# Attention and FFN block on one core: the second eight heads' q and k projected in their own batch, the next batch's norm begun nine turns later, the normalisation of attention on GpSimd

## The chip, the cores and the metric

The kernel runs on one core of a Trainium2 chip. The metric is device time in microseconds (us); a figure for a kernel is the median of several runs. A profile is one further execution, recorded instruction by instruction. The engines are TensorE (PE in the profile; its weight loads are PEld), VectorE (DVE), ScalarE (ACT), GpSimd (POOL) and SyncE (SP), which here only issues DMAs. Each engine works through its own instructions in the order in which the program wrote them, and waits where an operand or a buffer is not ready.

## The reference

Four sequences of 1024 tokens with 256 features go through an attention block and a gated FFN, each on a layer-normed input, and each result is layer-normed again before it is added:

```python
x = x + _layernorm(_L0_attn_ref(_layernorm(x), Wqkv, Wout))
x = x + _layernorm(_L0_ffn_ref(_layernorm(x), ...))

# attention, 16 heads of 16 features
qkv = (x @ Wqkv.T).reshape(B, S, 3, H, Dh)
scores = jnp.einsum('bhqd,bhkd->bhqk', q, k) * scale
exp_x = jnp.exp(jnp.clip(x - x_max, -50.0, 50.0))
attn = exp_x / (jnp.sum(exp_x, axis=-1, keepdims=True) + EPS)
out = jnp.einsum('bhqk,bhkd->bhqd', attn, v)      # then @ Wout.T

# FFN, 1024 hidden, ternary weights with a scale for each output
h = jax.nn.silu(_tlin(x, w1_w, w1_s)) * _tlin(x, w2_w, w2_s)
h = jax.nn.gelu(_tlin(h, h1_w, h1_s), approximate=False)
h = jax.nn.gelu(_tlin(h, h2_w, h2_s), approximate=False)
return _tlin(h, w3_w, w3_s)
```

All of it is float32.

## The kernel before

**Two stages.** Attention runs over all four batches first, then the FFN over eight halves of 512 tokens. The kernel is a fast path that assumes that scores stay small enough for a softmax without the maximum and that the FFN's weights are exact in a rounded float format. Both assumptions are tested on the way, and a slow path runs if one fails.

**Units, tiles, chunks.** A batch has 16 heads in four groups g of four. A group's queries are split in two halves h of 512; a group and a half make a unit. A unit is 16 tiles: eight chunks c of 128 keys, and for each chunk two tiles u of two heads each. A tile is two matmuls into PSUM (L457) and one exponential over 1024 elements on ScalarE (L458). When both tiles of a chunk are ready, four matmuls weigh the chunk (L465): they multiply the exponentials with the values and accumulate in `acc`. VectorE keeps a running maximum `top` of the first 128 queries' exponentials (L474), because the reference's EPS is scaled by it. There are 512 tiles in all, 128 in a batch.

**Turns.** The main loop (L874) goes by turns of three tiles. In each it makes up to three tiles, lets VectorE take up finished chunks into `top`, weighs one or two chunks whose exponentials are behind it, and then calls `side.take()` (L569) once. PSUM holds three tiles (pool `ps`, three buffers), so PE can be at most one turn ahead of ScalarE. At a unit's end (L600) VectorE copies `acc` to `o`, and the weighing of the next unit is put off to the next turn.

**Side work.** Everything else is cut into `Step`s in chains. `side.take()` goes over the chains in `first` and then in `rest`. Of each it takes steps from the front while `gap` turns have passed since that chain's last one. Only one step of a turn may use TensorE, and a chain whose next step would be the second waits. Nearly all of these steps share one PSUM buffer (`misc`, one buffer), which VectorE must have emptied before the next one.

The steps of attention are:

- `divide` (L476), once a unit, in `first`: transposes `top` and `o` on PE, then normalises on VectorE. It borrows one of the three score buffers, and the next turn makes a tile less at its start.
- `ending` (L501), appended to the unit's chain at the last group: two transposes of the result (`oT`), two output projections (`py`), two gathers of statistics, a root (the reciprocal root by a GpSimd `pow`, L103), two applies (L539, the normalisation (x - mean) * rstd, two instructions of 128x256 each), two residual additions (L546).
- `prologue` (L276) of the next batch: for each half, gathers and a root (lists `norm`), then two applies into `xn` (L302) and two transposes into `xT` (`xt`). After that come the q and k projections (L325), each 16 short matmuls and two evictions on VectorE, in two sets `qk[0]` and `qk[1]` for the first and the second eight heads (m = 0, 1). Then there are four steps `values` (`pv`). The steps `flags` test the scores' size: `total` (a reduction of 1024 elements on VectorE), `squares` (ScalarE, L344), `bound` (`pn`: four small matmuls and a reduction on VectorE, L367), `gauge` and `flag` (`pr`).
- `check_weights` (L236): loads a block of FFN weights on the GpSimd queue, rounds it on GpSimd (a cast of 128x1024), counts differences on VectorE, stores it.

**The order before.** `begin(b)` (L589) is called when batch b begins. It builds the whole prologue of batch b+1, and puts its norms, transposes and `qk[0]` in one chain, without delay except in batch 0. At the end of group 1, `unit_end` appends `values` to that chain, and adds a second chain that waits five turns and then does `qk[1]` and the flags. So both projection sets of batch b+1 are made while batch b runs, and `flags` runs over into batch b+1. Batch 0 also makes its own `qk[1]`, since before the loop only its `qk[0]` is made.

**Copies.** At a unit's end with h = 1, `stack` (L425) issues 32 DMAs of 64 KB on SP that lay out q and k of the group after next, and `slots` (L431) copies that group's values on GpSimd.

## Time and profile before

| | us |
|---|---|
| median of 3 runs | 1326.66 (1326.26 to 1327.31) |
| the profiled execution's own time | 1328.08 |
| its span, first to last instruction | 1326.3 |
| first exponential of batch 0 | 28.38 |
| last weighing of batch 3, about | 649.2 |

In the profiled execution TensorE was busy for 95% of the span, VectorE for 55%, ScalarE for 53% and GpSimd for 9%:

```profile
PE 1264.8 (95%) x8194; PEld 777.2 (59%) x8194; DVE 723.2 (55%) x1561; ACT 697.0 (53%) x847; POOL 120.5 (9%) x166
...
PE   7889999999999999889999999999999999999996
PEld 3333333333333333333478888888888888888885
DVE  3575669756696556646573543636436263362523
ACT  3687788877887787988641422414123141231410
POOL 5221112101121000000010000000000000000000
```

The rows below the dots cut the span in 40 equal slices (33 us each) and give the busy tenths of each. Attention is slices 1 to 20 and the FFN the rest. PE is nearly always busy, but a busy PE is not one at its peak: matmuls are pipelined and the profile models their ends. In attention ScalarE is at 7 to 9 tenths as well. A time by turns, read from ScalarE's rows, says more than these shares.

### The profile page before, as it was taken

To read this page: it belongs to the slowest core of one execution; us is meant where nothing else is said; L and a number is where in the kernel's file an instruction comes from. 1 tells how busy PE (TensorE), PEld (TensorE's weight loads), DVE (VectorE), ACT (ScalarE), POOL (GpSimd) and SP (SyncE) were. 2 spreads that over 40 slices of the span, in tenths; PEclk is the share of its full clock that TensorE was granted. 3 is DMA by queue.
4 is the path that set the end of the run, shared out by engine and by line. 5 is a ranking of instruction groups with operands and counts; after the bars stand their busy time and mean duration, and the time that the engine had idled before them with its cause. 6 is when DMAs were issued, how large, how long until landed. Compare 5 with 4: busy or idle time off the path is not lost.

```text
span 1326.3 us, 21103 instructions
## 1 busy us (share of the span) xinstructions
PE 1264.8 (95%) x8194; PEld 777.2 (59%) x8194; DVE 723.2 (55%) x1561; ACT 697.0 (53%) x847; POOL 120.5 (9%) x166
## 2 busy tenths in 40 slices
PE   7889999999999999889999999999999999999996
PEld 3333333333333333333478888888888888888885
DVE  3575669756696556646573543636436263362523
ACT  3687788877887787988641422414123141231410
POOL 5221112101121000000010000000000000000000
PEclk8999999999999999999999999999999999999998
DMA  4665444444444333334230000000000000000000
GB/s 127 156 184 128 102 97 116 118 112 121 105 110 110 68 64 65 59 63 166 81 112 0 1 16 1 17 0 6 11 0 17 0 17 0 0 17 0 17 0 20
DMA packets 38670, 79.76 MB, mean 60 GB/s; under 512 B 11296, under 2 KB 21152, under 8 KB 38560
## 3 DMA queue, kind: packets, MB, share of 16 engines
q1 hardware_dynamic: 30672, 53.66, 18.4%
q0 software_dynamic: 7360, 24.12, 5.6%
q8 instruction: 67, 1.10, 0.4%
q10 hardware_dynamic: 528, 0.52, 0.1%
q14 instruction: 43, 0.35, 0.1%
HBM read 28.98 MB, written 15.73 MB: 34 GB/s over the span
## 4 chain that ended last, share of the span: by engine, by line
PE 75%; DVE 12%; ACT 8%; issue 2%; DMA 1%; SPq 1%; ACTq 0%; POOL 0%; POOLq 0%; DVEq 0%
PE ph L703 35%; PE acc L465 12%; PE s L457 8%; ACT e L458 7%; PE pz L756 4%; PE p L268 4%; PE pg L703 4%; PE py L268 2%; DVE top L474 2%; PE pv L268 2%; DVE sg L719 2%; PE po L486 1%; DVE ha_lo L708 1%; DVE o L274 1%; DVE st L93 1%
## 5 line engine op out<-in xcount | busy, mean ns | idle before, releaser
L458 ACT ACTIVATE e<-s 128x1024 f32<-128x1024 f32 x512 | 486.3, 1035 | 121.7 <-PE s L457 109.0
L465 PE MATMUL acc<-e,vaug 128*32 128x512 f32 x2048 | 255.1, 600 | 1.4 <-POOL vaug L435 1.4
L739 ACT ACTIVATE a<-ph,h_scale 128x512 f32<-128x512 f32 x128 | 81.1, 686 | 306.9 <-PE ph L703 306.9
L457 PE MATMUL s<-sq,sk 64*128 64x512 f32 x1024 | 194.0, 449 | 25.5 <-ACT e L458 22.6
L703 PE MATMUL ph<-hb_lo,h 128*128 128x512 f32 x512 | 199.4, 389 | 0.0
L703 PE MATMUL ph<-hb_hi,h 128*128 128x512 f32 x512 | 199.4, 389 | 0.0
L457 PEld LDWEIGHTS s<-sq,sk 64*128 64x128 f32 x1024 | 86.6, 184 | 164.7 <-ACT e L458 126.9
L474 DVE TENSOR_TENSOR top<-top,e 128x512 f32<-128x512 f32 x192 | 133.6, 696 | 35.7 <-ACT e L458 30.2
L740 DVE CAST ha_hi<-a 128x512 fp32r<-128x512 f32 x64 | 27.1, 423 | 157.9 <-ACT a L739 157.9
L465 PEld LDWEIGHTS acc<-e,vaug 128*32 128x32 f32 x2048 | 49.2, 108 | 106.1 <-issue 97.3
L103 POOL TENSOR_TENSOR rstd<-ve,minus_half 128x4 f32<-128x4 f32 (+1 forms) x33 | 37.5, 1137 | 791.1 <-DVE ve L101 791.1
L703 PEld LDWEIGHTS ph<-hb_lo,h 128*128 128x128 f32 x512 | 96.1, 188 | 20.1
L703 PEld LDWEIGHTS ph<-hb_hi,h 128*128 128x128 f32 x512 | 96.1, 188 | 20.2
L703 PE MATMUL ph<-ha_hi,sq 128*128 128x512 f32 x256 | 101.9, 398 | 0.4
L703 PE MATMUL ph<-ha_lo,sq 128*128 128x512 f32 x256 | 99.9, 390 | 0.0
L703 PE MATMUL ph<-ha_lo,sk 128*128 128x512 f32 x256 | 99.8, 390 | 0.0
L703 PE MATMUL ph<-ha_hi,sk 128*128 128x512 f32 x256 | 99.7, 390 | 0.0
L719 DVE SCALAR_TENSOR_TENSOR sg<-pg,w_scale,sg 128x512 f32<-128x512 f32 x64 | 47.1, 745 | 48.4 <-ACT sg L717 48.4
L717 ACT ACTIVATE sg<-pg,w_scale 128x512 f32<-128x512 f32 x64 | 43.4, 689 | 57.2 <-DVE ha_lo L708 48.4
L740 DVE CAST hb_hi<-a 128x512 fp32r<-128x512 f32 x64 | 27.0, 422 | 82.3 <-ACT a L739 82.3
L268 PE MATMUL p<-xT,wqk_sb 128*32 128x512 f32 x512 | 62.3, 608 | 0.9 <-ACT xT L271 0.9
L703 PEld LDWEIGHTS ph<-ha_hi,sq 128*128 128x128 f32 x256 | 48.2, 188 | 12.7 <-DVE sg L719 3.4
(145 smaller groups left out, 1642.9 us busy)
## 6 DMA issues: line engine op xcount, KB each, us to landing
w<-in_h_dram POOLq DMA_DIRECT2D x16, 512.0 KB, 4.5
h_r<-wr POOLq DMA_DIRECT2D x16, 512.0 KB, 3.8
sk<-ck1hi SPq DMA_DIRECT2D x64, 64.0 KB, 2.3
sk<-ck1lo SPq DMA_DIRECT2D x64, 64.0 KB, 2.3
sq<-cq1hi SPq DMA_DIRECT2D x64, 64.0 KB, 2.3
sq<-cq1lo SPq DMA_DIRECT2D x64, 64.0 KB, 2.3
h<-h_r SPq DMA_DIRECT2D x8, 512.0 KB, 7.1
sk<-ck0hi SPq DMA_DIRECT2D x56, 64.0 KB, 2.3
```

The lines of the kernel that those rows point to most:

```text
L103: nc.gpsimd.tensor_tensor(rstd[:, :n], ve[:, :n], self.minus_half[:, :n], ALU.pow)
L268: nc.tensor.matmul(o[j : j + SLOT, :], w[:, j : j + SLOT], i, **flags)
L457: nc.tensor.matmul(s[:, a, :], stacks[1, g % 2, u][r, c * P : (c + 1) * P], stacks[0, g % 2, u][r, h * NQ : (h + 1) * NQ], start=True, sto ...
L458: nc.scalar.activation(pair(k)[:, u], s, AF.Exp)
L465: nc.tensor.matmul(acc[SLOT * i : SLOT * (i + 1), :], vaug[g % 2][:, c, i, :], pair(k)[:, i // 2, i % 2, :], start=c == 0, stop=c == NT - 1)
L474: nc.vector.tensor_max(top, top if c > 1 else pair(k - 2)[:, :, :, 0:P], pair(k)[:, :, :, 0:P])
L703: nc.tensor.matmul(p, homes[n][c][:, m * P : (m + 1) * P], half[:, c, :], start=c == 0 and k == 0, stop=c == len(homes[n]) - 1 and k == 1)
L717: nc.scalar.activation(sg, p[:, 0, :], AF.Silu, scale=scales["w1"][:, m : m + 1])
L719: nc.vector.scalar_tensor_tensor(sg, p[:, 1, :], scales["w2"][:, m : m + 1], sg, ALU.mult, ALU.mult)
L739: nc.scalar.activation(a, p[:, j, :], AF.Gelu, scale=scales[n][:, m : m + 1])
L740: nc.vector.tensor_copy(o[0][:, m, :], a)
L756: nc.tensor.matmul(p[t], half[:, c, t * P : (t + 1) * P], homes["w3"][c], start=c == 0 and k == 0, stop=c == HC - 1 and k == 1)
```

## The change

Three things are changed, and one follows from them.

1. **The second projections.** `prologue(b + 1)` is still built in `begin(b)`, but its `qk[1]` is kept in `own` and carried out when batch b+1 itself begins. It is a chain of four projections put in front of all others (`first=None`), two turns apart (one in batch 0). The chain's last step, `go_on`, then adds the flags of the second eight heads, and extends the chain of the next batch by its transposes, `qk[0]` and the flags of its first eight heads.
2. **The norm.** The chain of the next batch starts with nine turns of waiting instead of none (batch 0: four, as before), and does gathers and roots of both halves in a row. `values` has a chain of its own from the end of group 1, and the slots copy of the next batch's group 0 follows it where it is not done by then.
3. **The normalisation.** `Norms.apply` takes an engine. In `ending`, and in `prologue` of batches 1 to 3, the 128x256 instruction that subtracts and multiplies is issued on GpSimd; it was on VectorE.
4. **The flags** are split by m: `bound(m, h)` does two matmuls and a reduction over half of the partitions, so `pn` takes a PE step four times in a batch instead of twice. The small tiles `norm`, `sum` and `sum2` get two buffers.

```diff
-    def apply(self, o, t, stats, i):
+    def apply(self, o, t, stats, i, engine=None):
         mv, rstd = stats
-        self.nc.vector.tensor_scalar(o, t, mv[:, i, 0:1], rstd[:, i : i + 1], ALU.subtract, ALU.mult)
+        (engine or self.nc.vector).tensor_scalar(o, t, mv[:, i, 0:1], rstd[:, i : i + 1], ALU.subtract, ALU.mult)
...
-                        norms.apply(st["xn"][:, i, :], rows(h)[i], st["ln", h], i)
+                        norms.apply(st["xn"][:, i, :], rows(h)[i], st["ln", h], i, None if b == 0 else nc.gpsimd)
...
-            def bound(h):
+            def bound(m, h):
                 def run():
-                    pn = space(f"pn_{b}_{h}")
-                    for k, (w, m) in enumerate(kinds):
-                        nc.tensor.matmul(pn[SLOT * k : SLOT * (k + 1), :], heads_bf, st["sq", w, m], start=True, stop=True)
-                    nc.vector.tensor_reduce(st["norm"][:, TPQ * h : TPQ * (h + 1)], pn.rearrange("p (t n) -> p t n", n=P), AX.X, ALU.max)
+                    pn = space(f"pn_{b}_{m}_{h}")
+                    for w in range(2):
+                        nc.tensor.matmul(pn[SLOT * (2 * m + w) : SLOT * (2 * m + w + 1), :], heads_bf, st["sq", w, m], start=True, stop=True)
+                    own = slice(2 * SLOT * m, 2 * SLOT * (m + 1))
+                    nc.vector.tensor_reduce(st["norm"][own, TPQ * h : TPQ * (h + 1)], pn[own, :].rearrange("p (t n) -> p t n", n=P), AX.X, ALU.max)
...
-            flags = [Step(total(m), 1, False) for m in range(DC)]
-            for h in range(NH):
-                flags += [Step(squares(w, m, h), 1, False) for w, m in kinds] + [Step(bound(h), 1)]
-            return norm, xt, qk, v, flags + [Step(gauge, 0, False), Step(flag, 1)]
+            flags = []
+            for m in range(DC):
+                flags.append([Step(total(m), 1, False)])
+                for h in range(NH):
+                    flags[m] += [Step(squares(w, m, h), 1, False) for w in range(2)] + [Step(bound(m, h), 1)]
+            flags[-1] += [Step(gauge, 0, False), Step(flag, 1)]
+            return norm, xt, qk, v, flags
...
-                        norms.apply(st["y"][:, i, :], st["y"][:, i, :], st["ln"], i)
+                        norms.apply(st["y"][:, i, :], st["y"][:, i, :], st["ln"], i, nc.gpsimd)
...
-                (self.first if first else self.rest).append(chain)
+                if first is None:
+                    self.first.insert(0, chain)
+                else:
+                    (self.first if first else self.rest).append(chain)
                 return chain
...
-        def begin(b):
+        def begin(b, lead=()):
+            _, _, qk, _, flags = own.pop(b)
             if b + 1 < B:
-                norm, xt, qk, v, flags = prologue(b + 1, misc, to_vector)
-                qk1 = sum(qk[1], [])
-                qk1[0].gap = 3
-                later["rest"] = v, qk1 + [Step(lambda: side.add(flags), 0, False)]
-                later["chain"] = side.add([Step(lambda: None, 0 if b else 4, False)] + sum((norm[h] + xt[h] for h in range(NH)), []) + sum(qk[0], []))
+                own[b + 1] = prologue(b + 1, misc, to_vector)
+                norm, xt, qk_next, v, flags_next = own[b + 1]
+                later["chain"] = side.add([Step(lambda: None, 9 if b else 4, False)] + sum(norm, []))
+                later["v"] = v
+
+            def go_on():
+                side.add(flags[0] + flags[1] if b == 0 else flags[1])
+                if b + 1 < B:
+                    later["chain"][0].extend(sum(xt, []) + sum(qk_next[0], []) + flags_next[0])
+
+            left = sum(qk[1], [])
+            for step in left:
+                step.gap = 2 if b else 1
+            later["left"] = side.add(list(lead) + left + [Step(go_on, 0, False)], None)
...
                 stack(at, n)
-                slots(at, n)()
+                if at > b and later["v"]:
+                    assert n == 0
+                    later["v"].append(Step(slots(at, n), 0, False))
+                else:
+                    slots(at, n)()
             if g == NG - 3 and b + 1 < B:
-                v, qk1 = later["rest"]
-                assert not later["chain"][0]
-                later["chain"][0].extend(v)
-                side.add([Step(lambda: None, 5, False)] + qk1)
+                v = later["v"]
+                later["v"] = side.add(v)[0]
...
-        side.add(early + v[2:] + [Step(slots(0, 0), 0, False), Step(slots(0, 1), 0, False)] + sum(qk[1], []) + [Step(lambda: side.add(flags), 0, False)])
-        begin(0)
+        begin(0, early + v[2:] + [Step(slots(0, 0), 0, False), Step(slots(0, 1), 0, False)])
```

The rest of the difference adapts the final tests of the flags to the new layout of `pn`.

## The prediction

> **What bounds the kernel now.** I read the page first (engines, slices), then the windows of the four batches and of the FFN, then ScalarE's rows of the timeline turn by turn, then the groups and the waits of the engines that the change touches.

> The windows' boundaries are the starts of the first exponential of each batch; the columns are length, then busy time of PE, PE loads, VectorE (DVE), ScalarE (ACT), GpSimd (POOL).

> ```profile
> 28.38:192.48 164.10, 153.11 (x1302) 57.29 (x1306) 101.84 (x207) 127.20 (x141) 33.86 (x49) 0.99 0.55 134
> 192.48:351.93 159.45, 151.16 (x1301) 57.48 (x1296) 108.66 (x239) 125.26 (x138) 28.06 (x36) 1.00 0.48 112
> 351.93:507.92 155.99, 147.81 (x1258) 56.45 (x1252) 103.88 (x226) 124.92 (x137) 18.92 (x25) 1.00 0.41 88
> 507.92:649.20 141.28, 129.14 (x974) 47.22 (x972) 79.15 (x170) 122.49 (x132) 5.26 (x6) 1.00 0.38 83
> 649.20:1326.30 677.10, 662.28 (x3254) 550.47 (x3248) 318.36 (x684) 189.09 (x290) 19.50 (x18) 0.99 0.05 16
> ```

> The FFN (677.1 us) is PE work from end to end and the change hardly touches it. Attention takes 620.8 us. Batch 3, which prepares no successor, is 14.7 to 22.8 us shorter than the others though its exponentials are the same, so side work sets the difference. A few turns show how (start, length, count of exponentials; brackets hold the idle time before):

> ```profile
> 302.45 2.85 ACT L458 ACTIVATE e<-s 128x1024 f32<-128x1024 f32 x3 [1.20 <-PE s L457]
> 306.98 2.85 ACT L458 ACTIVATE e<-s 128x1024 f32<-128x1024 f32 x3 [1.68 <-PE s L457]
> 310.56 2.86 ACT L458 ACTIVATE e<-s 128x1024 f32<-128x1024 f32 x3 [0.72 <-PE s L457]
> ...
> 325.07 2.88 ACT L458 ACTIVATE e<-s 128x1024 f32<-128x1024 f32 x3
> 327.79 0.68 ACT L344 ACTIVATE sq<-cq1hi 128x512 bf16<-128x512 f32 x1
> 328.31 2.90 ACT L458 ACTIVATE e<-s 128x1024 f32<-128x1024 f32 x3
> ...
> 588.46 3.77 ACT L458 ACTIVATE e<-s 128x1024 f32<-128x1024 f32 x4 [0.58 <-PE s L457]
> 592.42 5.61 ACT L458 ACTIVATE e<-s 128x1024 f32<-128x1024 f32 x6 [0.19 <-PE s L457]
> ```

> From end to end of the third exponential, a turn with a projection takes 4.53 us (305.30 to 309.83) when two chunks are weighed in it and 3.59 when one is: PE decides. Two light turns take 5.80 together (592.23 to 598.03): exponentials decide in one, two chunks' weighing just beats them in the other. A light turn with a square takes 3.26 (327.95 to 331.21): ScalarE decides. Reading all 169 whole turns that way gives this table: q/k projection, values or output projection ("heavy") 3.58 with one chunk, 4.50 with two, 4.05 where a unit boundary splits the weighing; divide 4.25; light 2.75 with one chunk, 3.04 with two, 3.26 with a square; a four-block transpose 2.75, but 3.65 with two chunks, and 3.26 with a square; the flag's turn 2.85. The order of the built program says what stands in each turn. The table gives 607.0 for the 169 turns; they took 614.7. Of the 7.7 left, 2.7 lie in the first four turns and 2.6 in two divides of batch 0 (6.03 and 5.07 us instead of 4.25).

> [...] `top` takes 0.687 us in the median, but

> ```profile
> 341.60 1.24 POOL L251 CAST wr<-w 128x1024 fp32r<-128x1024 f32 x1 [3.33 <-DMA w<-in_h_dram]
> 341.98 1.41 DVE L474 TENSOR_TENSOR top<-top,e 128x512 f32<-128x512 f32 x1
> ...
> 344.04 1.93 PE L268 MATMUL py<-wo_sb,oT 128*32 128x256 f32 x32 [0.67 <-DVE oT L274]
> ```

> Here the eviction of oT behind `top` was late and PE lost 0.67 us. [...]

> **The change part by part.**

> ```profile
> L111 DVE TENSOR_SCALAR xn<-x,mv,rstd 128x256 f32<-128x256 f32 x24 | 10.1, 464 | 0.9 <-POOL rstd L103 0.9
> L111 DVE TENSOR_SCALAR y<-y,mv,rstd 128x256 f32<-128x256 f32 x24 | 10.2, 467 | 0.0
> L435 POOL COPY vaug<-cv 128x256 f32<-128x256 f32 x1 | 0.4, 397 | 0.3 <-DVE cv L274 0.3
> L356 POOL TENSOR_TENSOR sum<-sum 128x1 bf16<-128x1 f32 x8 | 4.6, 570 | 14.8 <-DVE sum L355 14.8
> ```

> (1) The move of the projections. The number of heavy turns does not change: 55 of 169 in either program; four projections leave batch 0, four arrive in batch 3, the middle batches swap theirs. Moving alone is worth nothing; what changes is which turn they share. Heavy turns, before: 10 at 4.05, 21 at 3.58, 24 at 4.50 = 223.7; after: 7, 24, 24 = 222.3. Divides: 31 at 4.25 in both. Transposes, before: 13 at 2.75, 3 with a square, 12 with two chunks = 89.3; after: 16, 1, 11 = 87.4. Light turns: the flags' bound is split by m, so `pn` takes 16 turns instead of 8 (the same matmuls, two in each), and the empty turns fall from 43 to 35. With squares first: 15 at 3.26, 10 at 3.04, 26 at 2.75, four flags = 162.2; after: 13, 11, 27, four = 161.5. More squares now stand in turns of `pv` and divides, where PE decides and their 0.65 us is hidden. Sum 606.9 to 602.9: minus 4.0 us. By batch: 158.0 to 151.4, 159.0 to 157.3, 156.0 to 155.1, 134.0 to 139.0.

> (2) The two late divides of batch 0. Both waited for `top` and `o` on a VectorE queue full of gather, count and total. In the new order the last projection stands in front of the first divide, which finds `o` and `top` a turn old, and no gather or total precedes the second. I take 2.0 of the 2.6 us. If VectorE's queue is merely late a turn further on, nothing is won: 0 to minus 2.6.

> (3) VectorE loses 48 normalisations in attention (20.3 us by the two rows) and 8 in the FFN's first turns, and gains 8 reductions of `pn` (0.684 us each, 5.5 us). It is 56% to 68% busy in these windows and PE hides most of it: nothing taken, minus 2 at best.

> (4) GpSimd gains 56 instructions of 256 elements. Below: the copy's 0.397 us. [...] I take 0.6, so 34 us. An apply step is then 1.2 us. For a batch's second half the applies may begin when xn is free, and PE comes to the transposes two turns and a weighing later: 2.75 + 3.04 + about 1.9 = 7.7 us for four instructions. They fit up to 1.9 us each, and nothing is taken for waits of PE. In the ending the residual stands two turns behind its apply. What queues behind an apply on GpSimd is the weights' load, cast and store (needed only in the FFN), the next pow, and the slots copy for a unit that begins ten turns later: hidden. An apply itself can stand behind a load that waits for VectorE's count of the same turn; it happens once before a transpose (batch 3's first half, turn 101), at most 0.5 us.

> (5) The lock. [...] three `top` were blocked, and two of them cost PE 0.67 and 0.69 us: 0.055 us per us held. 34 us more cost 1.9; four of the old normalisations had been blocked by casts themselves (up to 1.13 us), so I take 1.0. [...]

> (6) Norm nine turns later. gather, stats, aggr and ve are the same instructions and now miss the first ending, but meet the second ending and two divides that stand in or near adjacent turns (53 and 55, 96 and 97, 138 and 140). At the worst turn VectorE has two gathers (2.3 us), a divide (1.7), `o` (0.7), two ve (0.3) and `top` (about 0.9), 5.9 us in one of 4.3; the backlog is gone four turns on. I take plus 0.5; ends minus 1 and plus 2.

> SP's order is identical; the stack copies for heads 8 to 11 (2.3 us to landing) issue after the first group, when the last of these projections is at least one turn old.

> Sum: -4.0 - 2.0 + 1.0 + 0.5 = -4.5 us. The profiled execution would go from 1328.08 (span 1326.3 and 1.8 around it) to 1323.6. It stands 1.4 us above the median of the runs, 1326.66, so the median becomes 1322.1.

> **The rivals.** (B) No change: turns cost the same wherever the projections are, the prices by chunk count do not add up in new neighbourhoods, and the lock takes the rest[...]: 1326. For it: 55 heavy turns on both sides. Against: the prices repeat within 0.1 us.
> (C) Slower, GpSimd's price. If one normalisation takes more than 1.9 us, each of three second halves makes PE wait 4 times the excess, and the lock grows with it. At 2.2 us: 3 x 4 x 0.3 = 3.6, lock 123 us at 0.055 = 6.8, sum -4.0 - 2.0 + 0.5 + 10.4 = +4.9: 1331.5. For it: pow on four elements takes 1.14 us here. Against: copies and casts run at about 1 ns per element.
> (D) Faster than forecast: VectorE was the hidden limit in the endings. -4.0 - 2.6 - 2 - 1 + 0 = -9.6: 1317. For it: in the chain of waits within attention, `top` has 4.3% and `o` 2.6%. Against: PE waits for `top` 6.3 us and for `o` 4.9 us in all.

> **How the numbers follow.** Forecast 0.52 (1319 to 1324.5), B 0.22, C 0.14, D 0.12. The range leaves out the upper half of C and half of D: 1317.5 to 1328. 0.2% (2.65 us) is what a measurement of this kernel can tell. Faster: D and nearly all of the forecast, 0.63; within: B and a remainder, 0.22; slower 0.15.

> **What would show it.** Batch 0 shorter by some 8 us, batch 3 longer by some 5, the middle two shorter by 1 to 2; first divide near 4.3; an L111 row of GpSimd near 0.6 us; `pt` waiting on GpSimd under 2 us in all. It is wrong if batch 3 grows by as much as batch 0 shrinks, if the GpSimd row is over 1.9 us, or if `top`'s mean rises above 0.75 us with PE waiting behind it.

## The result, and the profile after

The changed kernel takes 1341.66 us (median of 4 runs, 1341.19 to 1341.99), beside 1326.99 (1326.26 to 1328.81) for the kernel before on the same chip: ratio 1.0108, 95% interval 1.0091 to 1.0126. It is 14.7 us slower, where 4.5 us less were forecast. Its profiled execution took 1341.19 us, span 1339.4.

The page first: the clock that PE was granted, in tenths of full speed and 40 slices, before; then the busy times of the engines, GpSimd's slices and the same clock row, after.

```profile
PEclk8999999999999999999999999999999999999998
```

```profile
PE 1275.0 (95%) x8194; PEld 782.6 (58%) x8194; DVE 715.4 (53%) x1517; ACT 697.3 (52%) x847; POOL 201.0 (15%) x222
...
POOL 6251113711326002200040000000000000000000
PEclk8999999999998999999999999999999999999998
```

GpSimd has 80.5 us more to do, VectorE only 7.8 less. PE's instructions are as many as before, but PE is busy 10.2 us longer: part of its work was done at a lower clock (slice 13 has an 8 where the kernel before has 9 from the second slice to the last but one).

The windows of the four batches and of the FFN, cut and laid out as for the kernel before:

```profile
26.03:184.85 158.82, 148.32 (x1242) 56.25 (x1246) 96.24 (x195) 127.07 (x140) 45.03 (x57) 0.99 0.57 139
184.85:348.45 163.60, 154.32 (x1300) 59.38 (x1292) 107.22 (x226) 124.99 (x138) 53.59 (x52) 0.98 0.48 109
348.45:513.18 164.73, 152.15 (x1258) 58.06 (x1256) 101.56 (x213) 125.61 (x137) 41.06 (x41) 0.98 0.39 83
513.18:657.80 144.62, 134.75 (x1034) 48.88 (x1032) 83.02 (x172) 122.58 (x132) 16.80 (x15) 1.00 0.37 81
657.80:1339.40 681.60, 664.73 (x3254) 551.84 (x3248) 316.08 (x676) 189.11 (x291) 29.84 (x26) 0.99 0.04 16
```

Batch 0 is 5.3 us shorter; batches 1, 2 and 3 are 4.1, 8.7 and 3.3 longer, and the FFN, which the prediction thought hardly touched, 4.5. The first exponential comes 2.35 earlier.

The group of the moved instruction (its columns: busy, mean ns of one | idle time ahead of it):

```profile
L111 POOL TENSOR_SCALAR y<-y,mv,rstd 128x256 f32<-128x256 f32 x32 | 44.7, 1404 | 0.6
L111 POOL TENSOR_SCALAR xn<-x,mv,rstd 128x256 f32<-128x256 f32 x24 | 35.8, 1497 | 11.1 <-issue 11.0
```

On GpSimd one normalisation takes 1.4 to 1.5 us in the mean, where VectorE took 0.46. The view of that line alone gives the spread and who waits, and the last row (PE's transposes of `xn`) parts these waits by engine:

```profile
L111 POOL TENSOR_SCALAR xn<-x,mv,rstd x24: 1211/1223/2789, 65.2 to 432.9; 128x256 f32<-128x256 f32 x24
...
  PEld pt L312: 14.2, 14
  PE pt L312: 7.0, 8
  DVE x L552: 5.7, 2
  PE fpt L716: 2.1, 1
...
L312 PE MATMUL pt<-ident,xn 128*128 128x128 f32 x64 | 13.5, 316 | 8.2 <-POOL xn L111 4.6 <-DVE xn L111 2.5 <-DVE norm L369 1.2
```

The three numbers are shortest, median and longest in ns: 1.21 us at the shortest, 2.79 at the longest. That longest one starts at 243.98, and VectorE runs `x<-x,y` and `top` beside it almost from its start to its end (busy for 2.68 of the 2.85 us from 243.95); step (5) below comes back to it. PE waits 7.0 us for `xn`, 4.6 of them for GpSimd's, where the prediction set under 2 us as its sign; the other 2.5 are for the start-up's `xn` on VectorE (the rows of PE and of its loads overlap and are not added).

Three places cost 5.1, 5.1 and 4.5 us, together as much as the whole loss; batch 0's gain pays for the smaller ones. First, batch 1 at the end of its second unit (timeline: start, length; brackets hold the idle time before it):

```profile
229.49 0.42 DVE L93 BATCH_NORM_STATS2 st<-y 128x6 f32<-128x256 f32 x1
...
230.77 0.42 DVE L93 BATCH_NORM_STATS2 st<-x 128x6 f32<-128x256 f32 x1
...
231.96 1.03 POOL L251 CAST wr<-w 128x1024 fp32r<-128x1024 f32 x1
231.97 1.05 DVE L101 TENSOR_SCALAR ve<-mv 128x4 f32<-128x4 f32 x1
232.93 0.68 DVE L480 TENSOR_TENSOR top<-top,e 128x512 f32<-128x512 f32 x1
...
233.76 1.09 PE L490 MATMUL po<-ident,top 128*128 128x128 f32 x4 [3.03 <-DVE top L480]
...
236.78 3.14 PE L471 MATMUL acc<-e,vaug 128*32 128x512 f32 x16
```

VectorE has the gathers of the ending (y) and of the next batch's norm (x) in one turn, then a four-element `ve` that takes 1.05 us beside a GpSimd cast (the median of `ve` is 0.17). `top` comes late, PE stands 3.03 us before the divide, and meanwhile its clock falls to half: 16 weighing matmuls take 3.14 us instead of 1.92. This is turn 55: 9.04 us, where turn 55 took 3.96 before.

Second, the first transpose of batch 3's `xn`, in turn 102, which takes 7.84 us and took 2.75 before:

```profile
406.86 1.02 POOL L103 TENSOR_TENSOR rstd<-ve,minus_half 128x4 f32<-128x4 f32 x1
407.89 3.52 POOL L111 TENSOR_SCALAR xn<-x,mv,rstd 128x256 f32<-128x256 f32 x2
411.27 0.52 PE L312 MATMUL pt<-ident,xn 128*128 128x128 f32 x2 [1.15 <-DVE norm L369]
411.36 0.65 POOL L259 DMA_DIRECT2D h_r<-wr  x1
412.01 0.53 POOL L247 DMA_DIRECT2D w<-in_h_dram  x1
412.58 2.43 POOL L111 TENSOR_SCALAR xn<-x,mv,rstd 128x256 f32<-128x256 f32 x2
413.86 0.47 PE L312 MATMUL pt<-ident,xn 128*128 128x128 f32 x1 [2.07 <-POOL xn L111]
```

From 407.89 to 415.01 four normalisations and two DMA issues follow one another on GpSimd, the first two beside VectorE's `top`, residual and count (3.52 us for the two, 2.43 for the others); PE has two of four blocks and waits for the others.

Third, the FFN, where the last ending still runs:

```profile
689.42 5.38 POOL L111 TENSOR_SCALAR y<-y,mv,rstd 128x256 f32<-128x256 f32 x4
...
694.84 0.69 DVE L552 TENSOR_TENSOR x<-x,y 128x512 f32<-128x512 f32 x1 [2.25 <-POOL y L111]
...
701.71 1.21 PE L716 MATMUL fpt<-ident,fxn 128*128 128x128 f32 x4 [2.06 <-DVE fxn L111]
```

Four normalisations in 5.38 us instead of VectorE's 1.38; the residual, the next tile's statistics and `fxn` are late by as much, and PE stands for 2.06 us.

The record of granted clock has half speed for 6.83 us at 232.5, 6.83 at 413.4 and 3.41 at 703.5, each during one of these waits or within 2 us of its end. In the profiled execution of the kernel before, there is none between start-up and the end.

### The profile page after: what moved, and what is told of

It reads as the page before. It is cut to its first block, busy times and chain, and to the rows that moved or that the text cites. A ratio compares the mean times of both kernels' runs of the same rounds, so it can differ in the third digit from the quotient of the medians.

```text
span 1339.4 us, 21115 instructions
## 1 busy us (share of the span) xinstructions
PE 1275.0 (95%) x8194; PEld 782.6 (58%) x8194; DVE 715.4 (53%) x1517; ACT 697.3 (52%) x847; POOL 201.0 (15%) x222
## 4 chain that ended last, share of the span: by engine, by line
PE 72%; DVE 10%; ACT 7%; POOL 4%; issue 4%; SPq 2%; DMA 1%; ACTq 0%; POOLq 0%; DVEq 0%
PE ph L727 34%; PE acc L471 12%; PE s L463 8%; ACT e L464 6%; PE pz L780 4%; PE p L268 3%; PE pg L727 3%; PE py L268 2%; PE pv L268 2%; DVE sg L743 2%; POOL y L111 2%; POOL xn L111 1%; DVE st L93 1%; SPq L425 1%; DVE top L480 1%
## 5 line engine op out<-in xcount | busy, mean ns | idle before, releaser
L480 DVE TENSOR_TENSOR top<-top,e 128x512 f32<-128x512 f32 x192 | 137.9, 718 | 27.7 <-ACT e L464 21.9
L103 POOL TENSOR_TENSOR rstd<-ve,minus_half 128x4 f32<-128x4 f32 (+1 forms) x33 | 37.3, 1132 | 765.2 <-DVE ve L101 765.1
L764 DVE CAST ha_hi<-a 128x512 fp32r<-128x512 f32 x64 | 27.1, 423 | 158.2 <-ACT a L763 158.2
L268 PE MATMUL p<-xT,wqk_sb 128*32 128x512 f32 x512 | 61.3, 600 | 1.2 <-ACT xT L271 0.9
```

What stands on the lines that cost most here:

```text
L268: nc.tensor.matmul(o[j : j + SLOT, :], w[:, j : j + SLOT], i, **flags)
L480: nc.vector.tensor_max(top, top if c > 1 else pair(k - 2)[:, :, :, 0:P], pair(k)[:, :, :, 0:P])
L764: nc.vector.tensor_copy(o[0][:, m, :], a)
```

## Experiments

Two readings stood against each other after the result. **G**: GpSimd's normalisation costs, by its length, by what it and VectorE lose beside each other ("the lock", step (5) below) and by its queue. **N**: what is left when VectorE normalises again costs, that is the moved and the later work itself, which meets endings and divides on VectorE. A third, **K**, came from the record of the clock. From e5 on, theory Q is the sharper form of N. This table is worked out from the windows of each profiled execution (lengths in us; FFN is the rest of the span); the ratio is against the kernel before in runs on the same chip, with its 95% interval.

| kernel | b 0 | b 1 | b 2 | b 3 | FFN | ratio |
|---|---|---|---|---|---|---|
| before | 164.1 | 159.4 | 156.0 | 141.3 | 677.1 | 1 |
| changed | 158.8 | 163.6 | 164.7 | 144.6 | 681.6 | 1.0108 (1.0091 to 1.0126) |
| e1 | 157.0 | 162.2 | 160.0 | 145.2 | 677.1 | 1.0022 (1.0014 to 1.0029) |
| e2 | 165.5 | 159.0 | 156.5 | 140.7 | 682.4 | 1.0034 (1.0021 to 1.0047) |
| e3 | 159.1 | 162.3 | 160.9 | 144.6 | 681.1 | 1.0076 (1.0056 to 1.0095) |
| e4 | 156.8 | 161.6 | 160.1 | 145.3 | 677.2 | 1.0015 (1.0005 to 1.0025) |
| e5 | 156.7 | 159.0 | 158.1 | 145.0 | 677.5 | 0.9963 (0.9951 to 0.9976) |
| e6 | 156.9 | 162.0 | 158.5 | 145.0 | 677.1 | 0.9986 (0.9979 to 0.9993) |
| e7 | 159.1 | 163.2 | 162.7 | 146.2 | 680.9 | 1.0085 (1.0069 to 1.0102) |
| e8 | 156.8 | 163.1 | 160.8 | 144.6 | 681.4 | 1.0045 (1.0028 to 1.0062) |
| e9 | 159.4 | 159.7 | 159.8 | 144.4 | 680.9 | 1.0030 (1.0019 to 1.0041) |
| e10 | 157.1 | 165.9 | 159.7 | 144.9 | 677.1 | 1.0047 (1.0030 to 1.0063) |
| e11 | 158.2 | 158.4 | 157.0 | 144.4 | 677.3 | 0.9966 (0.9953 to 0.9978) |
| e12 (e5 again) | 156.7 | 158.9 | 157.0 | 145.0 | 677.2 | 0.9977 (0.9968 to 0.9985) |

**e1 to e4: the parts apart.** e1 puts the normalisation back on VectorE and keeps the rest; e2 is the kernel before with GpSimd's normalisation alone; e3 is the change with the norm begun at once; e4 is e1 and e3 together, which leaves the move of the projections and the split flags.

```diff
# e1, e4: L304, then L545
-norms.apply(st["xn"][:, i, :], rows(h)[i], st["ln", h], i, None if b == 0 else nc.gpsimd)
+norms.apply(st["xn"][:, i, :], rows(h)[i], st["ln", h], i)
-norms.apply(st["y"][:, i, :], st["y"][:, i, :], st["ln"], i, nc.gpsimd)
+norms.apply(st["y"][:, i, :], st["y"][:, i, :], st["ln"], i)
# e3, e4
-later["chain"] = side.add([Step(lambda: None, 9 if b else 4, False)] + sum(norm, []))
+later["chain"] = side.add([Step(lambda: None, 0 if b else 4, False)] + sum(norm, []))
```

> The changed kernel with all normalisations back on VectorE; projections moved and norm nine turns late as changed. Theory G (the price of 1.22 to 2.8 us for a normalisation on GpSimd makes PE wait: the turns at tiles 33, 306, 309, 321 and the stall in the FFN, 13.5 us with the halved clock after them): 1326 to 1330 us. Theory N (the late norm falls on the second ending and overloads VectorE: the divides at tiles 165 and 291, 7 us with the clock): 1338 to 1343 us, since VectorE gets still more to do there. Both at work: between 1330 and 1336 us.

> The kernel before with nothing changed but the normalisations of the prologue of batches 1 to 3 and of the endings on GpSimd. Theory G: slower by 6 to 13 us, 1333 to 1340 us, with waits of PE for xn and the stall in the FFN's first layers. Theory N: within 2 us of before, 1325 to 1329 us.

> The changed kernel with the next batch's norm begun without the nine turns of waiting; GpSimd still normalises. Theory N: the divides at tiles 165 and 291 return to about 4.3 us, 1333 to 1336 us. Theory G: 1339 to 1343 us, as changed. If the waits for xn come from roots that are late themselves, they go too and the time falls below 1333 us.

> The changed kernel with both taken back: normalisations on VectorE and no nine turns of waiting, so only the move of the second projections (and the split flags) is left. If the prediction's first two terms hold (-4.0 for neighbours, -2.0 for the two divides of batch 0): 1319 to 1323 us. If the move itself costs time: above 1327 us.

1331.35, 1333.06, 1338.16 and 1330.25 us, where before took 1328.84. GpSimd is most of the loss: e1 is 0.86% below the changed kernel. But GpSimd alone on the old order (e2) costs 0.34%, and nearly all of that in the FFN (+5.3 of the profiled execution; attention +0.9). And the move alone (e4) doesn't gain: +0.15%. e1 lies in the range set for both theories together: G has the larger part, and the move isn't harmless either. e2 and e3 meet neither theory alone: e2 lost 4.2 us where G had 6 to 13 and N at most 2, e3 fell between N's 1336 and G's 1339. e4 is the case "the move itself costs time".

Where e4 loses: batch 0 and batch 3 do roughly what the price table says, batches 1 and 2 don't. Sorted by the kind of step in each turn (worked out from ScalarE's rows, as for the prediction's table), batches 1 and 2 together are 6.2 us longer than before: 4.3 in the turns of q, k, values and output projections, 2.5 in the divides, -0.6 in the rest. The projections now alternate with the endings' steps, and all of them need `misc` and VectorE: turn 47 takes 5.50 us (priced 4.50), turn 92, after a wait of PE of 1.19 us for `oT`, 4.95 (priced 4.05).

The divides of batch 2 show the same. In the kernel before, that of unit (2,0,0) stood in turn 92, five ahead of that of (2,0,1). The four projections, in front of all chains and every second turn, push the ending behind them, which closes at turn 95, and with it that divide to turn 96, next to the other in 97. VectorE in e4, and PE after it:

```profile
387.68 0.43 DVE L93 BATCH_NORM_STATS2 st<-y 128x6 f32<-128x256 f32 x1
...
388.77 0.66 DVE L494 TENSOR_REDUCE em<-po 128x4 f32<-128x512 f32 x1
...
390.36 0.68 DVE L257 SCALAR_TENSOR_TENSOR w<-w,wr 128x512 f32<-128x512 f32 x1
...
390.97 2.10 DVE L480 TENSOR_TENSOR top<-top,e 128x512 f32<-128x512 f32 x2
...
393.12 1.11 PE L490 MATMUL po<-ident,top 128*128 128x128 f32 x4 [2.70 <-DVE top L480]
```

Gather, the first divide's five operations (from `em` on), a count, and only then the `top` that the second divide needs: PE waits 2.70 us, and turn 97 takes 7.31. A half-speed stretch at 392.7 is in that figure.

**e5, e6, e12: the projections behind the endings.** In batches 1 to 3 the four projections are queued in front of the other side work, but behind the chains of endings and divides. e5 and e12 are one kernel, all on VectorE, norm at once; e6 begins the norm nine turns later.

```diff
 for step in left:
-    step.gap = 2 if b else 1
-later["left"] = side.add(list(lead) + left + [Step(go_on, 0, False)], None)
+    step.gap = 1
+if b:
+    later["left"] = [left + [Step(go_on, 0, False)], side.slot]
+    side.rest.insert(0, later["left"])
+else:
+    later["left"] = side.add(list(lead) + left + [Step(go_on, 0, False)], None)
```

> The changed kernel with every normalisation on VectorE, the norm chain begun without waiting, and, for batches 1 to 3, the four projections of heads 8 to 15 queued behind the endings' and divides' chain (in front of the other side work, one turn each) instead of in front of it. Theory Q (the move costs because the projections, put ahead of every other chain, push the first group's divides together and the endings' evictions behind one another): 1321 to 1325 us, 0.1% to 0.6% below the kernel before; the divide of unit (2,0,0) back near 4.3 us instead of 7.3; no half-clock stretch near 393 us. Theory M (having these projections at the head of the batch costs by itself, wherever exactly): 1328 to 1332, as with the projections in front. Theory P (the price table of the prediction is right but for the neighbours): at the lower end, 1321.

> The same order, with the norm chain begun nine turns later. Theory Q, with the late norm as costly as the pair on VectorE in front showed (+0.07%): within 1 us of the kernel without the waiting. If the late norm is what lets VectorE catch up in the endings: 1 to 3 us below it. If the late norm's gathers meet the second divides: 2 to 4 us above it.

> The version with the projections behind, all on VectorE, norm at once, once more beside the others: 0.9951 to 0.9976 against before if the first result stands.

1324.76 us for e5 (before 1329.69), 1325.47 for e12 (before 1328.46), 1327.70 for e6: the first two beat both kernels by Q's amount (e12, expected at 0.9951 to 0.9976, lies just outside with 0.9977). Batch 1 is back at 159, batch 2 at 157 to 158, and the divide of (2,0,0) is in turn 92 again. Q's details hold less well: that divide takes 5.19 us, not 4.3; turn 97 still takes 5.70 (e12) and 6.83 (e5); and e5 has a half-speed stretch at 389.3, which Q excluded. Between e4 and e5, both with such a stretch there, turn 97 differs by only 0.5 us. So it is shown that the place helps; keeping the two divides apart explains only a small part of it, and the rest is read from the waits and not tested. e6 is 0.23% above e5, as if the late gathers met the second divides, but only 0.09% above e12, with intervals that overlap: the cost of the late norm is small and not settled.

The pair e5 and e12 shows something else: one program (on two chips), the same wait in turn 97, and a clock that falls in one execution and not in the other. e5, then e12:

```profile
387.80 0.63 PE L490 MATMUL po<-ident,top 128*128 128x128 f32 x4 [1.75 <-DVE top L480]
...
389.70 1.93 PE L471 MATMUL acc<-e,vaug 128*32 128x512 f32 x8
```

```profile
388.61 0.63 PE L490 MATMUL po<-ident,top 128*128 128x128 f32 x4 [1.75 <-DVE top L480]
...
390.37 1.07 PE L471 MATMUL acc<-e,vaug 128*32 128x512 f32 x8
```

Eight weighing matmuls take 1.93 us in one and 1.07 in the other. e5's batch 2 is 1.16 us longer (158.15 and 156.99), and turn 97 alone makes 1.13 of it: the price of one such stretch of 3.4 us.

**e9, e10: place or spacing.** e9 is the changed kernel with the new place alone (the diff above). e10 is e4 with the four projections in front, but one a turn (`step.gap = 1`).

> The changed kernel in which only the place of the four projections in batches 1 to 3 differs: behind the endings' and divides' chain, one turn each. GpSimd still normalises, the norm still begins nine turns later. If GpSimd's price and the place add up: the kernel with the norm late and the projections behind measured 0.9986, and GpSimd cost 0.86% with the projections in front, so 1.007, about 1338 us where before takes 1329. If the place of the projections was also what made GpSimd's waits long: 1.000 to 1.004. If GpSimd's waits grow in the new order: 1.010 or more.

> Everything on VectorE, norm at once, the four projections in front of all other side work as in the changed kernel, but in four turns in a row instead of every second turn. Theory Q1 (it is the place behind the divides that makes the version with the projections behind faster): 1.001 to 1.004, no better than the same kernel with every second turn (1.0015). Theory Q2 (it is that they come in a row, so that the endings' chain is not interleaved with them): 0.996 to 0.998.

1332.46 and 1334.89 us, before 1328.46. e10 is worse than e4, so the place makes the gain, not the spacing (Q1, even beyond its numbers); beside e5 it differs only in the place. Pushed together, the endings' steps meet in turns 49 and 50, where PE waits 4.44 us for `o`. e9 is in the range of the second case: beside e6, GpSimd costs 0.44% here, and by windows 1.0 us in attention and 3.7 in the FFN. In the changed kernel, beside e1, it costs 7.3 in attention and 4.5 in the FFN. So the place of the projections also sets what GpSimd costs. The waits of PE for its `xn` shrink less, from 4.6 us to 3.7; by the stretches at half speed in attention (changed four of 3.41 us, e1 two, e9 one, e6 two) and 1.16 us for each, about 3.5 of the 6.3 us between 7.3 and 1.0 are clock (an estimate from single executions).

**e8, e11: which normalisation.** e8 is the changed kernel with `xn` back on VectorE, GpSimd only in the endings. e11 is e5 with y on GpSimd in batches 0 to 2 alone.

```diff
# e8 (to the changed kernel)
-norms.apply(st["xn"][:, i, :], rows(h)[i], st["ln", h], i, None if b == 0 else nc.gpsimd)
+norms.apply(st["xn"][:, i, :], rows(h)[i], st["ln", h], i)
# e11 (to e5)
-norms.apply(st["y"][:, i, :], st["y"][:, i, :], st["ln"], i)
+norms.apply(st["y"][:, i, :], st["y"][:, i, :], st["ln"], i, nc.gpsimd if b < B - 1 else None)
```

> The changed kernel with GpSimd normalising only y in the endings; xn of the next batch is normalised on VectorE again. Theory X (GpSimd's cost is PE waiting for xn under the lock, batches 1 and 2): 1333 to 1335, and batches 1 to 3 as with all on VectorE. Theory Y (it is the endings and the FFN's first tiles that wait for y): 1337 to 1341, with the FFN near 681 us. Equal shares: about 1336.

> The version with the projections behind and all on VectorE, but y of the endings of batches 0 to 2 normalised on GpSimd (the last batch's, beside which the FFN begins, stays on VectorE). If GpSimd's cost in the endings lay in the FFN's first tiles alone and relieving VectorE in the endings helps: 0.994 to 0.996 against before. If the lock and the later residual cost there too: 0.998 to 1.000. The FFN 677 us in either case.

1335.95 us (before 1329.69) and 1324.09 (before 1328.46). From e1 to e8, y adds 0.23% and the FFN goes to 681.4; from e8 to the changed kernel, `xn` adds 0.63%: 2.1 us in batch 0, 0.5 in batch 1, 3.9 in batch 2, none in batch 3, which prepares nobody. e8 fell where equal shares were expected; by the two steps both shares are real and `xn`'s is the larger. e11 lies between its two expectations, 0.1% from e12 with intervals that overlap: y on GpSimd costs nothing that could be told as long as the last batch, with the FFN behind it, is left out, and relieving VectorE in the endings was worth 0.1% at most.

**e7: the clock.** Three matmuls of 512 columns ahead of each of the three waiting PE steps, at these three places only (`transposes`, `divide`, and with other operands the FFN; the dots stand for lines left out):

```diff
+        def keep_busy(o):
+            for _ in range(3):
+                nc.tensor.matmul(o, ident, wo_sb.rearrange("p c d -> p (c d)"), start=True, stop=True)
...
+                    if (b, h, c) == (3, 0, 0):
+                        keep_busy(pt)
...
+                if (b, g, h) == (1, 0, 1):
+                    keep_busy(both[:, 0])
...
+                    if (n, c) == (1, 0):
+                        for _ in range(3):
+                            nc.tensor.matmul(pt, ident, xs[3].rearrange("p t d -> p (t d)")[:, 0:NQ], start=True, stop=True)
```

> The changed kernel with three extra matmuls of 512 columns in front of each of three PE steps that stand still in it (the first transpose of batch 3's xn, the divide of unit (1,0,1), the FFN's transpose of its second tile); their results are overwritten by the step itself, so this is about 2 us of extra PE work at each place and nothing of the computation changes. Theory K (the clock halves because PE stands still for over 2 us; 17 us at half speed in the changed kernel cost up to 8.5 us): 1333 to 1338 us, with no half-clock stretch at these places. Theory W (the waits alone cost, the clock follows something else): 1341 to 1346.

1340.84 us, ratio 1.0085: K's 1333 to 1338 is missed, and W's 1341 to 1346 narrowly too. The half-speed stretches at 232, 413 and 703 are gone, and the sum falls from 17.07 to 6.83 us: two new ones of 3.41 stand at 407.0 and 584.5. Turn 55 takes 6.56 instead of 9.04, turn 102 5.76 instead of 7.84, but turn 101, where the clock now falls, 4.38 instead of 2.75. And part of the gain goes to the wait that comes next, in e7 the transposes of `xn`:

```profile
244.20 6.91 POOL L111 TENSOR_SCALAR xn<-x,mv,rstd 128x256 f32<-128x256 f32 x4
...
249.96 0.33 PE L318 MATMUL pt<-ident,xn 128*128 128x128 f32 x1 [0.88 <-POOL xn L111]
...
251.16 0.33 PE L318 MATMUL pt<-ident,xn 128*128 128x128 f32 x1 [0.87 <-POOL xn L111]
```

Turn 59 goes to 5.47, 1.8 over its price, where the changed kernel, whose PE came later after the slow clock, took 3.53. Neither new stretch follows a long wait. Windows of e7, the 3.4 us ahead of the one at 584.5 and the 3.4 after (columns as above, PEclk before the last two):

```profile
581.10:584.50 3.40, 2.22 (x14) 0.71 (x14) 2.39 (x4) 3.40 (x5) 0.00 (x0) 1.00 0.00 0
584.50:587.90 3.40, 3.40 (x18) 0.94 (x12) 0.69 (x1) 1.89 (x3) 0.00 (x0) 0.50 0.37 63
```

PE was busy for 2.22 of 3.40 us, in light turns where ScalarE leads and no wait exceeds 0.42; it was the same before 407.0. So the clock is a surcharge, but not the cause: with three fifths of the half-speed time gone, e7 is 0.8 us faster in the median and 0.23% by the ratios, whose intervals overlap.

## Why the prediction was wrong, point by point

**Steps (1) and (2), the projections: right in two batches, wrong in two, and the sign lost.** With this part alone (e4), batch 0 is 7.3 us shorter (forecast 8.6 with the two divides) and batch 3 is 4.0 longer (forecast 5.0). The first divide took 4.65 us in the changed kernel, near the 4.3 announced. But batches 1 and 2 are 2.2 and 4.1 us longer where the steps said 1.7 and 0.9 shorter. The failing assumption is that a turn keeps its price by kind and chunk count whatever stands beside it: "Heavy turns" (223.7 to 222.3) and "Divides: 31 at 4.25 in both". Their numbers stay as counted, their neighbours don't: in these two batches heavy turns cost 4.3 us more than before and divides 2.5. A projection in front of all chains delays the divides and endings. Queued behind them (e5, e12), the same move gains 0.37% and 0.23%, about 3 to 5 us, of the 6.0 that steps (1) and (2) promised; batch 2 is still 1.0 us longer than before in e12. Which of the delayed steps carries the loss differs with the order: in e10, the slowest of these, the divides of batches 1 and 2 are cheaper than before (65.3 us, before 66.9) and the loss is in the turns of the endings' transposes.

**Step (3), VectorE's relief: not contradicted.** Nothing was taken, and e11 beside e12, which tests the endings' share only, finds 0.1% at most.

**Step (4), GpSimd: the term with the largest error**, 0.86% between e1 and the changed kernel where nothing was taken for waits of PE. Taken at 0.6 us, the instruction takes 1.22 undisturbed and 1.4 to 1.5 in the mean. The 0.6 was the author's estimate, set near the 0.397 us of a plain copy of 256 elements; no row of the kernel before has a subtract-and-multiply with two scalars on GpSimd. The sentence "They fit up to 1.9 us each" failed as well: it counted four instructions from the moment that xn is free, while root, ending's applies and DMA issues stand ahead of and between them on the same queue. Turn 101's "at most 0.5 us" was the right place and a tenth of the price: the transpose a turn later cost 5.1 us more than its turn had, half clock included. And only PE's waits in attention were asked for: the last ending's y delays the FFN's second tile, 3.7 to 5.3 us in every kernel that has it, old order or new. In e9, which has no half clock there, 2.6 us of 3.7 is PE idle between 690 and 700; the rest I have not located.

**Step (5), the lock: small on VectorE's side, not separated on the other.** The name stands here for what the traces show of the two engines beside each other. In the kernel before, the 22 casts took 24.8 us, and five `top` started during one: three took 1.02 to 1.41 us (median of all 0.687) and ended 0.54 us after the cast, the other two took 0.69, and one of these two casts took 1.74 us (median 1.04). What decides between these cases is not shown. In the changed kernel the mean of `top` rose from 0.696 to 0.718 us, 4.2 us over its 192 instructions, below the 0.75 set as a sign; but it is 0.709 in e1, where VectorE normalises, so only 1.8 of the 4.2 go with GpSimd's normalisations. On the other side, where the prediction didn't look, the excess is larger: the 56 normalisations on GpSimd took 80.5 us, 12 more than at 1.22 each, and the longest took 2.79 us instead of 1.21 beside `x<-x,y`, `top` and `x<-x,y` of VectorE in a row (0.68 us each, from 243.95). How much of the 12 is VectorE's doing is not separated: no run removes this effect alone.

**Step (6), norm later: right size where VectorE normalises, wrong with the rest.** e4 to e1 is 0.07%, within the intervals; e3 to the changed kernel 0.32%, about 4 us, with intervals that just touch. The step named turns 53 and 55, 96 and 97 and said that the backlog would be gone four turns on, for 0.5 us. The backlog is there, but `top` is in it, and PE needs it in the same turn: turn 55 alone took 5.1 us more. It does so with VectorE normalising too (7.91 in e1, 4.60 in e4), but e1 gets 2.3 us back in turns 43 to 52 (39.6, e4 41.9), which the gathers have left: there the late norm moves a collision more than it adds one.

**The rivals.** C (GpSimd's price) had the mechanism and the wrong threshold: it was to decide from 1.9 us on, and decides below it. None of the prediction's three signs of being wrong came true either (batch 3 grew by 3.3 where batch 0 shrank by 5.3, the GpSimd row stayed under 1.9 us, `top` under 0.75): it failed between them. B's 1326 was an estimate of the author's: the price that it set for the lock stands in no trace. What no rival had is the half clock. By the 1.16 us of e5 and e12, five stretches of 3.4 us would be some 6 of the 14.7 us (an estimate, if PE decides in all), and they are included in the shares above, not beside them.

Going from before by e4, e1 and e8 to the changed kernel, each beside its neighbour: move +0.15%, late norm +0.07%, y +0.23%, xn +0.63%; that they make 1.08% is so by construction. The kernel before had medians from 1326.99 to 1329.69 us in the four sets of runs, so steps of 0.2% between sets are not sure. The order of taking them apart matters: GpSimd costs 0.34% on the old order and 0.44% with the projections behind.

## What to carry to other kernels

Pricing side work by kind and count holds for the order that it was read from, not for a new one: when a chain is put in front, list every step that it delays, and look which of them now fall into one turn on the engine that all of them need. Before work goes to a slower engine (here 1.40 to 1.50 us in the mean on GpSimd, 0.46 on VectorE), lay out its whole queue from the producer to the waiting consumer, in the last iteration too, where the work beside it is another stage. Moving the four projections behind the divides turned +0.15% into -0.23% to -0.37%, with nothing else changed but their spacing, and e10 shows that the spacing was not what helped.

## What the runs showed of the hardware

The runs of the kernel before, on three chips, give the price of a unit once more: the 39 with a granted clock of 0.991 have a median of 1329.87 us, the 8 with 0.994 one of 1326.84. A clock lower by 0.003 is 2.3 units of 3.41 us in 1327, so a unit costs about 1.3 us (an estimate; a straight line through each chip's runs gives 1.1 to 1.2), near the 1.16 above. The same wait of 1.75 us thus went with about 1.1 us more in e5 and with none in e12.
